# Loads of one weight moved to ScalarE's queue, and two fill products in place of five

## The chip, the cores and the metric

The kernel runs on one core of a Trainium2 chip. The metric is device time in microseconds (us) for one execution, taken from three runs of the same kernel. Five engines work beside each other: TensorE (PE in the profile, with its weight loads shown as PEld), VectorE (DVE), ScalarE (ACT), GpSimd (POOL) and SyncE (SP), which here only issues DMAs. DMAs can be issued by SP, by ACT and by POOL; a row such as "SPq ... DMA_DIRECT2D" in a timeline is the issue, not the transfer.

## The reference

For 8 samples of 1024 rows with 512 features, two conditioned residual layers follow each other:

```python
# layer 0: a base matrix plus a low-rank term made from the condition
ae = layernorm(cond) * ln_g + ln_b
h = gelu(ae @ w1 + b1)
x_a, x_b = split(h @ w2 + b2, 2)              # each (8, 512, 8)
layer = base[None] + einsum('bdr,bkr->bdk', x_a, x_b)
x = x + (x + einsum('btc,bco->bto', x, layer))
# layer 1: a weight scaled by the condition on its rows and normalised on its columns
ys = cond / sqrt(512)
d = rsqrt(einsum('bi,io->bo', ys * ys, W * W) + 1e-8)
x = x + einsum('bsi,io->bso', x * ys[:, None, :], W) * d[:, None, :]
```

The kernel multiplies the two layers into one 512 x 512 matrix for each sample and then applies that matrix once to x. For this it needs products of base (plus twice the identity) with W, scaled for each sample.

## The kernel before

Products are made in a 32-bit form that drops low bits, so each operand is split into a rounded part and a rest (`bh` and `bl` for base, an `nh` and an `nl` for W scaled by `ysT`), and each block product is the sum of three matrix products. Blocks are 128 rows; the inner dimension of 512 has four chunks, k = 0 to 3.

The setup comes first and the main stage after it. The setup makes the scaled norm `d`, the condition's layer norm `ae`, the small network (`w1`, then sixteen tiles of `w2`, 1 MB each, summed into `px`), the first base product `pg` for sample 0 and base products for samples 1 to 3. The main stage runs over 8 samples and 8 row blocks each; each step is twelve matrix products into `po`, a copy by ScalarE and a store issued by ScalarE. The base products and splits of later samples are woven between these steps.

The order of the setup is written out by hand. `mm` and `turn` (lines 44 to 48) pin TensorE's products and transposes to program order, and `ve`, `se` and `sy` (line 64) do the same for VectorE, ScalarE and SyncE. An engine that waits for one operand therefore holds back all that stands behind it.

The loads stand at lines 86 to 92, all on SyncE: `sm` (identity, the layer norm's parameters, the transposed condition: 86 KB), `cnd` (the condition, 16 KB), then by halves of 512 KB W (`w_sb`) and base transposed (`b_raw`) in turn, then `w1` (1 MB). The tiles of `w2` follow from `w2_group` (line 387), each of which issues a load ahead of four products; nine large buffers are shared (`big`, line 69), so later tiles wait until earlier buffers are free. Loads from SP and ACT share a small set of completion semaphores in program order; a load that takes a semaphore over waits until the earlier load with it has landed.

`keep_warm(count)` (line 106) issues products of a zero tile into a PSUM tile that nobody reads. Twelve of them (`WARM`) start the program on TensorE at line 111. Five more stand at line 256, between the transposes `pa` of the normalised condition and the first base products.

For the first base product (lines 257 to 259) these must be there: the first half of W, scaled and rounded by ScalarE (`round_yw`, lines 179 and 186, which stand behind ScalarE's square root of the layer norm at line 178); the first half of base, with twice the identity added by VectorE (`twice_i`, line 187) and then rounded, a quarter by VectorE (line 188) and three quarters by ScalarE (line 189).

Of the kernel before, what the change touches and what calls it, by code (L numbers as in the profile page):

```python
# [30 lines left out]
def cond_resid_kernel(ctx: ExitStack, tc: tile.TileContext, small, cond, condrows, consts,  # L31
# [10 lines left out]
    nc = tc.nc  # L42

    def mm(*args, **kw):
        tc.keep_in_program_order(nc.tensor.matmul(*args, **kw))  # L45

    def turn(*args):
        tc.keep_in_program_order(nc.tensor.transpose(*args))

    pin = tc.keep_in_program_order  # L50
# [13 lines left out]
    ve, se, sy = InOrder(nc.vector), InOrder(nc.scalar), InOrder(nc.sync)  # L64
# [16 lines left out]
    w_sb = cp.tile([P, KC, D], F32, name="w_sb")  # L81
# [4 lines left out]
    sy.dma_start(sm, small)  # L86
    sy.dma_start(cnd, cond)
    for at in (slice(0, 2), slice(2, 4)):
        sy.dma_start(w_sb[:, at, :], weight[:, at, :])
        sy.dma_start(b_raw[:, at, :], baseT[:, at, :])  # L90
    w1_sb = big_tile("w1_sb")
    sy.dma_start(w1_sb, w1)
# [13 lines left out]
    def keep_warm(count):  # L106
        for _ in range(count):
            mm(warm.rearrange("p (a c) -> p a c", c=P), zero,
               zero.unsqueeze(1).to_broadcast([P, D // P, P]), start=True, stop=True)
# [143 lines left out]
    pa = misc.tile([P, KC, NB], F32, tag="misc", name="pa")  # L253
    for k in range(KC):
        turn(pa[:, k, :], ae[:, k * P:(k + 1) * P], ident[:NB, :NB])
    keep_warm(5)
    for i, (s, m) in enumerate(((bh, n0[0][0]), (bh, n0[0][1]), (bl, n0[0][0]))):
        for c in range(KC):
            mm(pg[c], s[:, 0, c * P:(c + 1) * P], m, start=(i == 0), stop=False)
# [672 lines left out]
```

## Time and profile before

| | us |
|---|---|
| median of three runs | 305.82 |
| lowest and highest | 305.3 and 306.11 |
| the profiled execution | 305.47 |
| its span, from the first to the last instruction | 303.7 |

The span is cut into forty slices in the page. Busy shares are in tenths (9 is 90% or more), and the last two rows give the DMA engines' busy share and what they moved in GB/s:

```profile
PE   8999999999999999999999999999999999999995
DVE  4779830979678479977456478981266543600000
ACT  4756132256476564355664454743645546621221
DMA  6999999642319636631651134354151545322222
```

A slice is 7.6 us. TensorE is busy in all of them. The DMA engines are busy in the first seven or so, while the weights are loaded, and partly idle afterwards. The page's table of DMA issues names the loads around the change; its last column is the median time from issue to landing:

```profile
w<-in_w SPq DMA_DIRECT2D x16, 1024.0 KB, 11.1
...
w_sb<-in_weight SPq DMA_DIRECT2D x2, 512.0 KB, 5.4
b_raw<-in_baseT SPq DMA_DIRECT2D x2, 512.0 KB, 6.2
w_sb<-in_w SPq DMA_DIRECT2D x1, 1024.0 KB, 9.6
```

The sixteen rows named `w<-in_w` are the tiles of `w2`. The row `w_sb<-in_w` is the load of `w1`, whose name the profile gives in part only. In the rows of a timeline the first column is the start, the second the duration, and brackets hold the idle time of that engine just before and what ended it.

### The profile page before, as it was taken

How to read it: one execution, taken by the hardware profiler on the slowest of the kernel's cores; microseconds unless marked ns; L12 is line 12 of the kernel's file. 1: busy time of each engine (PE TensorE's matmuls, PEld its weight loads, DVE VectorE, ACT ScalarE, POOL GpSimd, SP SyncE). 2: the span in 40 equal slices, each digit the busy share in tenths (PEclk: the TensorE clock that was granted, in tenths of full speed). 3: DMA queues.
4: the chain of work that ended last, by engine and by line, in shares of the span. 5: the costliest groups of instructions: out<-in, count | busy, mean ns of one | idle time of the engine just before them, and what ended most of it. 6: DMA issues, size and time to landing. Idle time of an engine off the chain costs nothing.

```text
span 303.7 us, 3551 instructions
## 1 busy us (share of the span) xinstructions
PE 298.0 (98%) x1369; PEld 227.9 (75%) x1369; DVE 176.4 (58%) x262; ACT 145.9 (48%) x212; POOL 5.2 (2%) x14
## 2 busy tenths in 40 slices
PE   8999999999999999999999999999999999999995
PEld 3655565466888888888888888888888888888884
DVE  4779830979678479977456478981266543600000
ACT  4756132256476564355664454743645546621221
POOL 0011000001000000100000000000000000000000
PEclk9999999999999999999999999999999999999999
DMA  6999999642319636631651134354151545322222
GB/s 204 409 427 419 410 421 419 220 188 69 138 69 343 242 124 226 228 120 69 207 193 52 69 108 171 97 162 192 69 207 69 190 178 212 148 106 104 96 76 105
DMA packets 15952, 57.37 MB, mean 189 GB/s; under 512 B 1840, under 2 KB 2352, under 8 KB 11584
## 3 DMA queue, kind: packets, MB, share of 16 engines
q1 hardware_dynamic: 6064, 38.78, 34.5%
q10 hardware_dynamic: 9360, 16.78, 14.7%
q0 software_dynamic: 512, 1.59, 1.6%
q8 instruction: 10, 0.16, 0.2%
q14 instruction: 6, 0.05, 0.1%
HBM read 40.35 MB, written 16.79 MB: 188 GB/s over the span
## 4 chain that ended last, share of the span: by engine, by line
PE 88%; DVE 5%; DMA 4%; ACT 2%; issue 0%; ACTq 0%
PE po L45 57%; PE pp L45 13%; PE pq L45 7%; DMA w<-in_w 4%; PE px L45 3%; PE warm L45 2%; PE pg L45 2%; DVE n L62 2%; PE pr L45 2%; PE pt_t L45 1%; ACT work L62 1%; DVE scr L62 0%; PE ps_t L45 0%; DVE q L62 0%; PE pq_v L45 0%
## 5 line engine op out<-in xcount | busy, mean ns | idle before, releaser
L45 PE MATMUL po<-ph,xs 128*128 128x512 f32 (+1 forms) x520 | 164.2, 386 | 0.0
L45 PEld LDWEIGHTS po<-ph,xs 128*128 128x128 f32 x520 | 97.1, 188 | 19.8
L45 PE MATMUL po<-pl,xs 128*128 128x512 f32 (+1 forms) x260 | 100.3, 386 | 0.0
L62 ACT COPY o<-po 128x512 f32<-128x512 f32 (+1 forms) x65 | 37.8, 581 | 87.0 <-PE po L45 86.8
L45 PEld LDWEIGHTS po<-pl,xs 128*128 128x128 f32 x260 | 48.8, 188 | 9.9
L62 DVE TENSOR_TENSOR xs<-x,xs 128x1024 fp32r<-128x1024 f32 x32 | 38.7, 1221 | 20.5 <-ACT xs L62 20.5
L62 ACT CAST xs<-x 128x1024 fp32r<-128x1024 f32 x32 | 33.0, 1050 | 4.0 <-DMA x<-in_x 2.3
L62 DVE TENSOR_TENSOR nl_p<-n,nh_p 128x1024 fp32r<-128x1024 f32 x14 | 17.1, 1220 | 20.0 <-ACT nh_p L62 20.0
L62 DVE TENSOR_TENSOR pl<-q,ph 128x1024 fp32r<-128x1024 f32 x16 | 19.4, 1220 | 7.3 <-ACT ph L62 7.3
L62 DVE TENSOR_TENSOR q<-pr,q 128x512 f32<-128x512 f32 x24 | 15.8, 685 | 7.9 <-PE pr L45 7.8
L45 PE MATMUL pq<-nh,bh 128*128 128x512 f32 x48 | 19.8, 412 | 0.0
L45 PE MATMUL pq<-nl,bh 128*128 128x512 f32 x48 | 19.1, 398 | 0.1
L45 PE MATMUL pq<-nh,bl 128*128 128x512 f32 x48 | 19.0, 395 | 0.0
L62 ACT CAST ph<-q 128x1024 fp32r<-128x1024 f32 x16 | 16.6, 1051 | 3.9 <-DVE q L62 3.7
L62 DVE SCALAR_TENSOR_TENSOR n<-w_sb,ysT,d 128x512 f32<-128x512 f32 x24 | 17.8, 745 | 0.8 <-DMA d<-d_out 0.8
L62 ACT COPY q<-pp 128x512 f32<-128x512 f32 x20 | 11.7, 587 | 13.3 <-PE pp L45 13.3
L45 PE MATMUL px<-w,hT 128*32 128x512 f32 x128 | 16.0, 601 | 0.4 <-DMA w<-in_w 0.4
L62 ACT CAST nh_p<-n 128x1024 fp32r<-128x1024 f32 x14 | 14.7, 1052 | 2.5 <-PE pp L45 2.4
L45 PEld LDWEIGHTS pq<-nh,bh 128*128 128x128 f32 x48 | 9.0, 188 | 8.4 <-issue 5.0
L45 PE MATMUL pp<-nh_p,sh 128*128 128x512 f32 x32 | 12.4, 389 | 0.0
L45 PE MATMUL pp<-nl_p,sh 128*128 128x512 f32 x32 | 12.4, 389 | 0.0
L45 PE MATMUL pp<-nh_p,sl 128*128 128x512 f32 x32 | 12.4, 389 | 0.0
(135 smaller groups left out, 272.9 us busy)
## 6 DMA issues: line engine op xcount, KB each, us to landing
w<-in_w SPq DMA_DIRECT2D x16, 1024.0 KB, 11.1
x<-in_x SPq DMA_DIRECT2D x16, 1024.0 KB, 5.2
out<-o ACTq DMA_DIRECT2D x63, 256.0 KB, 2.0
d<-d_out POOLq DMA_DIRECT2D x6, 256.0 KB, 3.9
w_sb<-in_weight SPq DMA_DIRECT2D x2, 512.0 KB, 5.4
b_raw<-in_baseT SPq DMA_DIRECT2D x2, 512.0 KB, 6.2
w_sb<-in_w SPq DMA_DIRECT2D x1, 1024.0 KB, 9.6
b_nat<-in_base SPq DMA_DIRECT2D x1, 1024.0 KB, 9.5
```

What stands on the lines that cost most here:

```text
L45: tc.keep_in_program_order(nc.tensor.matmul(*args, **kw))
L62: return lambda *a, **kw: pin(f(*a, **kw)) if InOrder.on else f(*a, **kw)
```

## The change

The two loads of W are issued on ScalarE's queue, where they become its first instructions, in front of its table load. SyncE's queue keeps the small loads, base, `w1` and `w2` in the same order without W. The fill in front of the first base product has two products instead of five. Everything else, the order on VectorE and the rest of the order on TensorE included, stays.

```diff
     sy.dma_start(sm, small)
     sy.dma_start(cnd, cond)
     for at in (slice(0, 2), slice(2, 4)):
-        sy.dma_start(w_sb[:, at, :], weight[:, at, :])
+        pin(nc.scalar.dma_start(w_sb[:, at, :], weight[:, at, :]))
         sy.dma_start(b_raw[:, at, :], baseT[:, at, :])
     w1_sb = big_tile("w1_sb")
     sy.dma_start(w1_sb, w1)
...
         turn(pa[:, k, :], ae[:, k * P:(k + 1) * P], ident[:NB, :NB])
-    keep_warm(5)
+    keep_warm(2)
     for i, (s, m) in enumerate(((bh, n0[0][0]), (bh, n0[0][1]), (bl, n0[0][0]))):
```

Two semaphores move with it: W's first half takes the one that the small load had, and the load of the constants (`cst`, behind `w2`'s first tile on SyncE) now waits for that half of W where it waited for the small load.

## The prediction

> **What bounds the kernel now.** I read the page's busy shares first: TensorE is the bound, so only what moves TensorE's work earlier or later can count.
>
> ```profile
> PE 298.0 (98%) x1369; PEld 227.9 (75%) x1369; DVE 176.4 (58%) x262; ACT 145.9 (48%) x212; POOL 5.2 (2%) x14
> ```
>
> Of 303.7 us, TensorE sits idle for 5.7. Second, the list of waits of PE, to see where that idle time lies (columns: total us, times, longest us):
>
> ```profile
> PE warm L45 <- DVE eps_l L62: 1.0, 1, 1.0
> PE px L45 <- DMA w<-in_w: 0.4, 1, 0.4
> PE pd L45 <- DVE dst L62: 0.4, 1, 0.4
> ```
>
> One DMA wait in the whole run. Third, the timeline of 0 to 60 us, for what releases the first base product and for that wait:
>
> ```profile
> 1.57 0.35 SPq L62 DMA_DIRECT2D w_sb<-in_weight  x1
> 1.97 0.43 SPq L62 DMA_DIRECT2D b_raw<-in_baseT  x1
> ...
> 5.45 1.33 ACT L62 ACTIVATE nh<-w_sb,ysT 128x512 fp32r<-128x512 f32 x2 [1.44 <-DMA w_sb<-in_weight]
> ...
> 6.26 1.25 PE L45 MATMUL warm<-zero 128*128 128x512 bf16 x5
> 6.78 0.51 ACT L62 CAST bh<-b_raw 128x384 fp32r<-128x384 f32 x1
> 6.78 0.29 DVE L62 SCALAR_TENSOR_TENSOR b_raw<-sm,b_raw 128x128 f32<-128x128 f32 x1 [1.30 <-DMA b_raw<-in_baseT]
> ...
> 7.44 0.76 PEld L45 LDWEIGHTS pg<-nh,bh 128*128 128x128 f32 x4 [0.42 <-ACT bh L62]
> ...
> 48.03 1.06 PE L45 MATMUL px<-w,hT 128*32 128x512 f32 x8 [0.43 <-DMA w<-in_w]
> ```
>
> The first half of base (b0) lands at 6.78, ScalarE's rounding ends at 7.29, the first product's weights load at 7.44. ScalarE's own previous work (two roundings of W, from 5.45) also ends at 6.78, so both halves arrive together. The five fill products end at the same moment, 7.5: at present none of the three is slack. From 7.44 on TensorE is dense; at 48.03 it waits 0.43 us for a tile of w2 (the eleventh). Fourth, the windows, for the DMA stream (last two columns: DMA share, GB/s):
>
> ```profile
> 1.50:2.50 1.00, 1.00 (x4) 0.35 (x3) 0.00 (x0) 0.72 (x2) 0.00 (x0) 1.00 0.39 105
> 2.50:4.50 2.00, 2.00 (x6) 0.73 (x5) 1.49 (x7) 0.29 (x1) 0.00 (x0) 1.00 0.82 217
> 4.50:6.25 1.75, 1.75 (x9) 0.66 (x7) 0.87 (x4) 0.81 (x2) 0.00 (x0) 1.00 1.03 407
> 6.25:7.75 1.50, 1.50 (x8) 0.71 (x7) 0.94 (x4) 1.22 (x3) 0.00 (x0) 1.00 0.93 224
> ...
> 10.00:48.00 38.00, 37.08 (x207) 20.72 (x205) 26.27 (x60) 17.43 (x33) 2.53 (x5) 1.00 1.02 419
> ```
>
> From 10 to 48 us the stream runs full at 419 GB/s, so the tile awaited at 48.03 comes earlier only if the whole stream starts earlier. At the start there is room: up to 2.5 us just 105 KB move, which are the two small loads (86 + 16 KB); W's first half (W0), issued at 1.57, starts some 0.95 us after its issue.
>
> **What the Trainium skill says.** "DMA: Bandwidth & Descriptors", section "Issuing engines are not separate DMA queues": loads of SP and ACT run on the same 16 engines and interleave; several issuers save only issue time. The trace agrees for the full part (one queue alone reaches 419 GB/s), so I expect an earlier start, not a higher rate. The section "Queues, rings and completion order" of the same page: each engine takes turns between the two rings. The trace agrees only in part. A store of ACT issued 0.01 us after an x load landed with it; one issued 0.5 us after an x load landed after it had finished (both against 2.0 us for stores on their own):
>
> ```profile
> x<-in_x SPq DMA_DIRECT2D x1, 1024.0 KB, 5.6
> out<-o ACTq DMA_DIRECT2D x1, 256.0 KB, 5.8
> ```
>
> ```profile
> x<-in_x SPq DMA_DIRECT2D x1, 1024.0 KB, 5.2
> out<-o ACTq DMA_DIRECT2D x1, 256.0 KB, 5.4
> ```
>
> "Perfetto Trace Analysis", section "DMA Instruction — HWDGE (DVE, Sync)": the descriptor generator is shared and locked for one issuer. No issue in this trace shows a long lock wait (at 90.5 both queues issue together in 0.33 and 0.36 us). "TensorE: Matmul & The Clock Gate", "What's actually happening": an idle window of about 3.4 us drops the clock. The granted clock is 1.00 in all windows above; no gap in this trace is long enough to show it.
>
> **The change, part by part.** Call d the time by which the first base product comes earlier, and e the same for the DMA stream. At 48.03 the product of w2 starts at the later of TensorE's arrival (47.60 - d) and the tile (48.03 - e). After it TensorE is dense to the end (0.24 us idle from 60 to 290). So the gain is the smaller of 0.43 + d and e.
>
> *Three fill products removed.* 1.25 us / 5 = 0.25 each, 0.75 together. TensorE is then free at 6.26 + 0.50 = 6.76 instead of 7.51. Worth nothing if base is not earlier; it caps d at 7.44 - 6.76 = 0.68, and the gain at 0.43 + 0.68 = 1.11.
>
> *ScalarE's two issues.* Each some 0.35 to 0.43 (the rows of W and base on SP), in front of its table load (1.28 us from 0.74) and one small activation (0.20): that ends at about 1.5 + 1.28 + 0.20 = 3.0 instead of 2.23. Its next work is at 3.71, so 0.7 us of cover; cost 0.
>
> *e.* W0 is issued at 0.74 in place of 1.57: the stream starts 0.83 earlier. Lower bound 0.4 (if the generator takes the two small loads' issues, 0.37 each, in turn with W's); upper 1.3 (if the slow stretch 2.50 to 4.50, which loses 2.0 x (419 - 217)/419 = 0.96 us, halves because both tensors start together). I take 0.83. Later SP loads all move up too; consts now waits for the semaphore that W0 frees instead of the small load's, perhaps 0.3 us later than its issue at 4.76, and two loads of 1 MB, 5 us, are queued ahead of it: cost 0.
>
> *d, by base.* On SP b0 moves from 1.97 to 1.57, but W1 is now issued near 1.1, ahead of it. At best b0 follows the stream, 0.83 earlier, and the cap 0.68 holds. At worst all 512 KB of W1 pass first, as with the store issued 0.5 us late: 524 KB / 413 GB/s = 1.27 us, so b0 is 1.27 - 0.83 = 0.44 later.
>
> *d, by cond.* The small loads now share with W0. Cond stands behind up to 512 KB: at best 0, at worst 1.3 us. The layer norm follows it step by step (2.79 to 5.47), then the transposes pa (0.35), which precede the two fills. At present pa waits for the warm-up products until 5.91, 0.4 us after its operand, so a delay of 1.3 makes it 0.9 late: 6.76 + 0.9 = 7.66 for the first product, d = -0.2. ScalarE's square root waits too, but W0 covers it.
>
> So d lies between -0.44 and 0.68; I take the middle, +0.1. The gain: the smaller of 0.43 + 0.1 and 0.83, 0.53. Profiled execution: 305.47 - 0.53 = 304.94 (its span of 303.7 and 1.8 around it). The median of the three runs is 0.35 above that execution, so 305.3 on its scale. What is late next: at 48 TensorE itself again.
>
> **Rivals.**
> 1. *All cover holds, faster.* The small loads keep their turn and b0 comes with the earlier stream: d = 0.68, e at least 1.1, gain 1.1: 304.7. For it: the empty DMA before 2.5 us. Against: it needs e at its upper part, and no delay by W1.
> 2. *Base becomes the late one, slower.* b0 becomes the third half-megabyte instead of the second. The third load now, W1, was issued at 2.43 with 6.9 us to landing: 9.33. Less 0.83, b0 lands at 8.5, 1.7 later: d = -1.7, gain 0.43 - 1.7 = -1.3: 307.1. It decides as slower once b0 is later than 6.78 + 1.35 = 8.1. For it: the slow stretch 6.25 to 7.75 at 224 GB/s, which b0 escapes today. Against: nothing shows that this stretch belongs to the third place. A clock dropped in the then empty 1.7 us would add to it.
> 3. *The stream does not start earlier.* The generator takes issues in turn, e = 0.4 or less: gain 0 to 0.4, 305.4 to 305.8, no change.
>
> **How the numbers follow.** 0.3% is 0.92 us, about what a measurement of this kernel can tell. The forecast (gain -0.2 to 0.9) 0.36, rival 1 0.32, rival 2 0.22, rival 3 0.10. Rival 1 stands on the threshold, so a little more may fall beyond it from the forecast's upper end: faster 0.34, same 0.44, slower 0.22. Predicted 305.3. The forecast's own range is 304.9 to 306.0; with rival 1 less 0.2 for scatter 304.5, and up to most of rival 2, 307.0.
>
> **What would show it.** Right: W0's issue on ACT at 0.74; DMA over 200 GB/s before 2.5 us; the wait at 48 gone or under 0.4; the first base product near 7.3. For rival 1, that product at 6.8. For rival 2, base's wait on DVE ending past 8, a gap of TensorE after the two fills, and the 48 us product later than 48.03. Cond's statistics on VectorE (now 2.79) show how the small loads fared. Wrong altogether if TensorE shows a new wait after 60 us, or a clock below 1.00.

## The result, and the profile after

The changed kernel takes 308.0 us (median of six runs, 306.99 to 308.35) against 305.25 for the kernel before beside it: a ratio of 1.0077, interval 1.0058 to 1.0096. It is slower by 2.75 us, where 305.3 with a range of 304.5 to 307.0 was predicted. The profiled execution took 308.35, with a span of 306.4 against 303.7.

The page's busy shares and clock row for the changed kernel:

```profile
PE 298.7 (97%) x1366; PEld 228.6 (75%) x1366; DVE 176.4 (58%) x262; ACT 145.7 (48%) x212; POOL 5.1 (2%) x14
...
PEclk9799999999999999999999999999999999999999
```

The clock row of before:

```profile
PEclk9999999999999999999999999999999999999999
```

TensorE does three products fewer and is busy for 0.7 us more. The 7 in the second slice says that its clock was not full there; before, that row held nines only. TensorE's waits in the changed kernel (total us, times, longest):

```profile
PE pa L48 <- DVE scr L62: 2.0, 1, 2.0
PE warm L45 <- DVE eps_l L62: 1.0, 1, 1.0
PE pd L45 <- DVE dst L62: 0.3, 1, 0.3
PE pr L45 <- DVE q L62: 0.3, 1, 0.3
PE pg L45 <- DVE bh L62: 0.2, 1, 0.2
```

The wait for a tile of w2 is gone. In its place TensorE waits 2.0 us for the normalised condition, ahead of the fills, and 0.2 for base, behind them. The timeline of the changed kernel at its start, with issues on the two queues:

```profile
0.74 0.37 SPq L62 DMA_DIRECT2D sm<-in_small  x1
0.74 0.88 ACTq L89 DMA_DIRECT2D w_sb<-in_weight  x2
...
3.97 0.18 DVE L62 TENSOR_SCALAR ysT<-sm 128x32 f32<-128x32 f32 x1 [3.03 <-DMA sm<-in_small]
...
4.87 0.68 DVE L62 BATCH_NORM_STATS2 st<-scr 8x6 f32<-8x512 f32 x1 [0.72 <-DMA scr<-in_cond]
...
7.62 0.41 PE L48 MATMUL pa<-sm,scr 8*128 8x8 f32 x4 [1.95 <-DVE scr L62]
7.96 0.73 PE L45 MATMUL warm<-zero 128*128 128x512 bf16 x2
8.22 0.51 ACT L62 CAST bh<-b_raw 128x384 fp32r<-128x384 f32 x1 [0.91 <-DMA b_raw<-in_baseT]
...
8.92 2.05 PE L45 MATMUL pg<-nh,bh 128*128 128x512 f32 x4 [0.23 <-DVE bh L62]
```

The rows of before that these are read against, beside the rows of base in the prediction:

```profile
2.69 0.18 DVE L62 TENSOR_SCALAR ysT<-sm 128x32 f32<-128x32 f32 x1 [1.75 <-DMA sm<-in_small]
2.79 0.68 DVE L62 BATCH_NORM_STATS2 st<-scr 8x6 f32<-8x512 f32 x1
...
5.92 0.41 PE L48 MATMUL pa<-sm,scr 8*128 8x8 f32 x4
...
7.47 1.16 PE L45 MATMUL pg<-nh,bh 128*128 128x512 f32 x4
```

The small load reaches VectorE at 3.97 (2.69 before), cond at 4.87 (2.79), the transposes `pa` run at 7.62 (5.92), base lands at 8.22 (6.78), and the first base products start at 8.92 (7.47). Those four then take 2.05 us where they took 1.16. Windows of the changed kernel show why (length, busy time by engine, then clock, DMA share, GB/s); they are cut where the clock changed, and the first has the same length as the second:

```profile
4.90:8.31 3.41, 1.46 (x10) 0.58 (x8) 2.33 (x10) 1.61 (x4) 0.00 (x0) 1.00 0.98 359
8.31:11.73 3.42, 3.19 (x9) 2.27 (x8) 3.39 (x9) 3.14 (x7) 0.00 (x0) 0.50 1.04 438
11.73:15.00 3.27, 3.27 (x17) 2.18 (x19) 2.80 (x7) 1.85 (x3) 0.16 (x1) 1.00 1.01 416
```

In the first window TensorE was busy for 1.46 of 3.41 us, and for the next 3.42 it ran at half clock. How late TensorE was further on is read from two more products, `pq_v` behind the base products and the last one of the run, first before and then changed:

```profile
11.82 1.07 PE L45 MATMUL pq_v<-wsq,ysq 128*32 128x512 f32 x8
...
299.93 0.28 PE L45 MATMUL po<-ph,xs 128*128 128x256 f32 x1
```

```profile
14.56 1.07 PE L45 MATMUL pq_v<-wsq,ysq 128*32 128x512 f32 x8
...
302.40 0.28 PE L45 MATMUL po<-ph,xs 128*128 128x256 f32 x1
```

From the first base product to `pq_v` it took 11.82 - 7.47 = 4.35 us before, and now 14.56 - 8.92 = 5.64: 1.29 more. So TensorE was 1.45 late by the first base product and 2.74 late at `pq_v`. The wait of 0.43 at the w2 tile, which is gone, gives that much back. In the last matrix product of the run the lag is 302.40 - 299.93 = 2.47 us.

### The profile page after: what moved, and what is told of

The parts are those of the page before. It is cut to its first block, busy times and chain, and to the rows that moved or that the text cites. A ratio compares the mean times of both kernels' runs of the same rounds, so it can differ in the third digit from the quotient of the medians.

```text
span 306.4 us, 3545 instructions
## 1 busy us (share of the span) xinstructions
PE 298.7 (97%) x1366; PEld 228.6 (75%) x1366; DVE 176.4 (58%) x262; ACT 145.7 (48%) x212; POOL 5.1 (2%) x14
## 4 chain that ended last, share of the span: by engine, by line
PE 89%; DVE 5%; DMA 2%; ACT 1%; issue 1%; SPq 0%; ACTq 0%
PE po L45 57%; PE pp L45 13%; PE pq L45 9%; PE px L45 4%; PE pg L45 2%; DMA b_raw<-in_baseT 2%; DVE n L62 2%; PE pr L45 2%; PE pt_t L45 1%; ACT work L62 1%; DVE scr L62 0%; PE ps_t L45 0%; DVE q L62 0%; PE pq_v L45 0%; ACT nh L62 0%
## 5 line engine op out<-in xcount | busy, mean ns | idle before, releaser
L62 ACT CAST nh<-n 128x512 fp32r<-128x512 f32 (+1 forms) x10 | 6.9, 708 | 12.9 <-DVE n L62 12.9
```

Source lines behind the costliest of these rows:

```text
L62: return lambda *a, **kw: pin(f(*a, **kw)) if InOrder.on else f(*a, **kw)
```

## The experiments

My theory after the result, A: a load issued about 0.4 us later than another waits for all of that one's packets, on whichever queue; cond thus stands behind the first half of W, base behind both halves, and the wait for cond leaves TensorE idle enough for its clock to halve. The rivals were the removed fills, the use of two queues in itself, and an early issue on ScalarE.

**Each part alone.** The loads on ScalarE's queue with five fills kept:

```diff
-    keep_warm(2)
+    keep_warm(5)
```

> The loads of W on ScalarE's queue, all five fill products kept. Theory A (issue order: cond stands behind the first half of W, base behind both halves, and TensorE's clock halves while it waits for cond): the fills are not what costs; the statistics start near 4.9 us, base lands near 8.2, the clock drops all the same, and the three extra fills run at half clock in front of a base that has come, so 308 to 309 us, 1.0 to 1.2% above the kernel before. Theory B (the clock drops because three fills were taken out): clock at full, first product near 8.9, 306.7 us or less.

Measured: 309.62 us, ratio 1.0128 (1.0106 to 1.0151), somewhat above the range of A; B falls. The windows of this run (same columns) show the clock at half for twice as long:

```profile
4.03:7.44 3.41, 1.21 (x6) 0.35 (x4) 2.10 (x10) 1.43 (x3) 0.00 (x0) 1.00 0.98 365
7.44:10.85 3.41, 3.02 (x10) 1.75 (x11) 2.94 (x8) 2.45 (x6) 0.00 (x0) 0.50 1.02 428
10.85:14.27 3.42, 3.42 (x9) 2.64 (x8) 3.39 (x10) 2.71 (x5) 0.00 (x0) 0.50 1.02 424
```

The five fills ran at half clock from 8.36 and pushed the first base products to 10.11, although base had landed at 8.21. With these loads, fewer fills are the better choice: 308.0 against 309.6.

The fills alone, with all loads on SyncE as before:

```diff
-    keep_warm(5)
+    keep_warm(2)
```

> All loads on SyncE, two fill products in place of five. Theory A: TensorE stands idle for some 0.7 us in front of the first base product and nothing else moves: first product at 7.4, time within 0.3% of before. Theory B: the clock drops here too, 1.3 us or more lost, 306.6 us or above.

Measured: 305.1 us, ratio 1.0003 (0.9989 to 1.0018). The time is as A expects, although base itself came later in this trace (7.03) and the first base product at 7.73 after a wait of 0.52. With the loads in their old order the fills cost and gain nothing that can be told from none, so the loss comes with the loads.

**The clock's share.** The changed kernel with TensorE kept busy from the start until cond is there:

```diff
-WARM = 12
+WARM = 19
```

> The changed kernel with 19 instead of 12 products of zeros at the very start, so that TensorE is busy until cond's transposes can begin (near 7.6 us). Theory A: no second stretch at half clock; the late base alone remains, first product near 8.9, 1.45 later than before, less the 0.43 us wait at 48: 306.3 to 306.7 us, some 1.3 below the changed kernel. Theory C (the clock's dip costs nothing, the late base is all): 308 as the changed kernel.

Measured: 306.89 us, ratio 1.0052 (1.0037 to 1.0066): 1.1 below the changed kernel, with the clock at 1.00 in the window that ran at half clock there. The two rows show TensorE busy through the window before, and then the clock, for this run:

```profile
4.90:8.31 3.41, 3.41 (x14) 1.25 (x13) 2.52 (x10) 1.78 (x4) 0.00 (x0) 1.00 1.03 394
8.31:11.73 3.42, 3.42 (x19) 2.72 (x19) 3.39 (x9) 3.14 (x7) 0.00 (x0) 1.00 1.02 432
```

It is a little above the range of A, but C falls. Of the remaining 1.6 us (0.5%), the trace shows TensorE 1.28 late at the first base products (8.75) and 1.12 late at its last product (301.05 against 299.93); what the rest is stays open. The changed kernel's own runs show the same split: the one whose mean clock was 0.998 took 306.99, the five with 0.992 or 0.993 took 307.81 to 308.35.

**What makes base late.** The second half of W goes back to SyncE, behind base's first half:

```diff
-        pin(nc.scalar.dma_start(w_sb[:, at, :], weight[:, at, :]))
+        by = se if at.start == 0 else sy
+        by.dma_start(w_sb[:, at, :], weight[:, at, :])
```

> As the changed kernel (two fills), but only the first half of W on ScalarE's queue; the second half goes back to SyncE, behind the first half of base. Theory A (a load issued later waits for what the other queue issued before): base has only the first half of W ahead of it and lands 1.2 to 1.4 us earlier than in the changed kernel, near 6.9; cond is as late as there (statistics near 4.9), so the transposes stay near 7.6, the first base product comes near 8.3, the clock still drops: 307.2 to 307.7 us. Theory E (the two queues share by turns, and base is late for another reason): base still lands near 8.2, 308 us.

Measured: 307.7 us, ratio 1.0078 (1.0056 to 1.01). The first base load's row in the table of DMA issues, of the changed kernel and of this run (last column: us to landing), issued at 1.58 and 1.57:

```profile
b_raw<-in_baseT SPq DMA_DIRECT2D x1, 512.0 KB, 6.6
```

```profile
b_raw<-in_baseT SPq DMA_DIRECT2D x1, 512.0 KB, 4.8
```

Base lands 1.8 us sooner after its issue with nothing moved but the second half of W: E falls. Cond stays late (statistics at 4.94), `pa` stays at 7.68, and the first base products start at 8.28. In the profiled execution the clock held, and it is the lowest of fourteen times (306.08 to 310.14); the clock had risen later there (the twelve warm-up products took 5.30 us, against 4.68 in the changed kernel), so that the wait for cond was shorter, 1.4 us. The median, 307.7 against 308.0, says that base alone repaired gains little as long as cond is late.

**What makes cond late.** One queue only, the first half of W issued first:

```diff
+    sy.dma_start(w_sb[:, first, :], weight[:, first, :])
     sy.dma_start(sm, small)
     sy.dma_start(cnd, cond)
     sy.dma_start(b_raw[:, first, :], baseT[:, first, :])
+    sy.dma_start(w_sb[:, second, :], weight[:, second, :])
```

> All loads on SyncE and five fills as before, but the first half of W is issued ahead of the two small loads. Theory A (order of issue alone makes cond late, whichever queue): the small loads land behind the first half of W, statistics at 4.5 us or later, transposes at 7.3 or later, the clock drops: 307 to 309 us although base is in its old place. Theory F (two queues beside each other are what hurts): statistics below 3.5, time within 0.3% of before.

Measured: 308.3 us, ratio 1.0088 (1.0057 to 1.0119), with this timeline:

```profile
5.01 0.18 DVE L62 TENSOR_SCALAR ysT<-sm 128x32 f32<-128x32 f32 x1 [4.07 <-DMA sm<-in_small]
5.10 0.68 DVE L62 BATCH_NORM_STATS2 st<-scr 8x6 f32<-8x512 f32 x1
...
7.84 0.41 PE L48 MATMUL pa<-sm,scr 8*128 8x8 f32 x4 [1.60 <-DVE scr L62]
```

Cond is as late, and the loss as large, without ScalarE's queue. So it is the order of issue and not the second queue: F falls. Then the changed kernel with its two small loads exchanged:

```diff
-    sy.dma_start(sm, small)
     sy.dma_start(cnd, cond)
+    sy.dma_start(sm, small)
```

> The changed kernel with the two small loads on SyncE in the other order, cond (one packet on each of eight DMA engines) ahead of the 86 KB load (eight packets on each engine). Theory A with turns (each DMA engine takes packets of the two queues in turn while both were issued together, and what is issued later waits): cond lands with the first packets of W, the 86 KB load as late as before or a little later (scaling at 4.0 to 4.3); the statistics follow the scaling at 4.2 to 4.5 in place of 4.87, the transposes come near 7.1, and base stays last near 8.2: 307 to 308 us, the clock drops in fewer executions. Theory G (all small loads wait until the first half of W is through): statistics at 4.8 or later again, 308 us or more.

Measured: 308.47 us, ratio 1.0109 (1.0072 to 1.0146). The numbers are those of G, but neither theory had the mechanism right. What SyncE's queue (q1) moved from 1.60 to 2.40 us (packets, MB, share of 16 engines), and the rows for the 86 KB load, issued at 1.19 behind W's issue at 0.74:

```profile
q1 hardware_dynamic: 16, 0.02, 13.8%
...
sm<-in_small SPq DMA_DIRECT2D x1, 86.0 KB, 4.1
...
5.29 0.18 DVE L62 TENSOR_SCALAR ysT<-sm 128x32 f32<-128x32 f32 x1 [4.35 <-DMA sm<-in_small]
5.38 0.67 DVE L62 BATCH_NORM_STATS2 st<-scr 8x6 f32<-8x512 f32 x1
```

Cond was there: the 0.02 MB are its 16 KB, moved before 2.40, and the statistics ran 0.09 us after the scaling, with no wait for a DMA. But VectorE takes the scaling first, and the 86 KB load, now the later one, took 4.1 us from its issue. In the changed kernel, issued in the same moment as W, it took 3.2, and before, with nothing ahead of it, 1.9. So a load issued 0.45 us later did not share with the earlier one packet by packet; it waited for nearly all of it.

**A way to keep the early start.** Only the 16 KB load of cond goes to ScalarE's queue, so that nothing large comes ahead of a small load and W is issued 0.4 us earlier:

```diff
-    sy.dma_start(cnd, cond)
+    pin(nc.scalar.dma_start(cnd, cond))
```

> The kernel before with only the 16 KB load of cond on ScalarE's queue; W, base and five fills as before. Theory A: cond arrives beside the other small load, ahead of W; W and all that follows on SyncE are issued 0.4 us earlier, the tile of w2 awaited at 48 comes 0.4 earlier: 304.9 us, 0.1% faster (0 to 0.2%). Theory D (any load issued first by ScalarE delays the start, through its table load): statistics later than 2.8, first product later than 7.44, time above before by 0.3 us or more.

Measured: 306.69 us, ratio 1.0044 (1.0026 to 1.0062), with times from 305.23 to 309.6. D's numbers came true (statistics at 2.93, the first base products at 8.61, 1.4 us lost), but its mechanism is not shown: the run with the fills alone has its statistics at 2.93 too, with all loads on SyncE. What was late is the first half of W: it took until 6.20, where it was there at 5.45 before, although issued 0.40 us earlier. A repetition on another chip:

> The kernel with only cond on ScalarE's queue a second time, for a second trace and more times on another chip. Theory D (an early load on ScalarE's queue makes the start of the stream slower): median again 0.3% or more above before, first half of W landing at 6.0 or later, first base product at 8.3 or later. Theory H (the first trace showed one of the stream's slow starts, which before has too): median within 0.2% of before.

Measured: 306.14 us, ratio 1.0028 (1.0008 to 1.0048); W at 6.09, first base products at 8.03. That lies between D and H. The w2 tile came later too: TensorE waited for it until 48.95. The traces cannot decide: the run with the late base copy, below, starts with its loads in the old order, and in its trace W comes at 6.07 and the first base products at 8.03 as well. The loss is measured in the times of both runs (42 executions); its cause stays open. Issuing W earlier did not move its arrival forward in either.

**Two tries at a faster kernel.** First, the wait at 48 us taken away, by loading the second copy of base (1 MB) one w2 tile later:

```diff
-        if len(todo) == 6:
+        if len(todo) == 5:
```

> The kernel before, with one edit: the 1 MB load of base for the later addition is issued after the eleventh tile of w2 instead of ahead of it. By the sum of the prediction the gain is the smaller of 0.43 + d and e; here d = 0 and e = 2.5 us (1 MB at 419 GB/s), so the wait at 48 goes and 0.0 to 0.43 us are gained: 304.9 us, 0.1%. If the addition then waits for its base (used at 55.8), the gain is lost: 305.3 or above.

Measured: 305.65 us, ratio 1.0001 (0.9986 to 1.0016). There was no wait for w2 in its profile, and no gain that could be told from none. But TensorE was itself 0.56 late at the first base products there (8.03), so the trace does not show that the edit took the wait away. The wait is not in each execution of the old order either: the run with two fills alone had none, and its tile was used from 47.79 on, 0.24 earlier than in the trace of before. Then with W and base in quarters and two fills on top:

```diff
-    for at in (slice(0, 2), slice(2, 4)):
+    for at in (slice(0, 1), slice(1, 2), slice(2, 4)):
...
-    keep_warm(5)
+    keep_warm(2)
```

ScalarE and VectorE do the first quarter's work ahead of the second's in that kernel.

> The edit of the run before it (late base copy), all loads on SyncE, the first halves of W and base loaded in quarters in turn (W0, base0, W1, base1), ScalarE's and VectorE's work on the first quarter ahead of the second, two fills. By the prediction's sum d = 0.5 to 0.68 with e = 2.5: gain 0.9 to 1.1 us, first base product at 6.8 to 7.0, 304.3 us, 0.3% faster. Rival: two more issues on SyncE and smaller packets slow the slow start of the stream further, base's second quarter comes after 7.5 and holds the products of k = 1: no gain, 305.3.

Measured: 305.46 us, ratio 0.999 (0.9974 to 1.0005), no clear gain. In its profiled execution, which took 306.94, the first base products started at 7.49 only, and the window from 2.50 to 4.50 us moved 130 GB/s, where the kernel before moved 217, which is the slower start that the rival named. No kernel here beats the one before by more than its interval.

## Why the prediction was wrong

*The form held, two terms did not.* The gain was written as the smaller of 0.43 + d and e. The first step that failed is the size of d, taken as +0.1 between -0.44 and 0.68: the first base product came 1.45 later. The second is the clock, which was read as 1.00 and priced at nothing: it cost 1.29 us between that product and `pq_v`. With both, the sum is 0.43 - 1.45 - 1.29 = -2.31. The lag at the last product is 2.47; most of the difference comes at a later product `pr`, where TensorE now waits 0.28 us for VectorE and the lag grows from 2.31 to 2.44.

*The stream, e.* The windows of the changed kernel, and the one of before that the prediction does not show:

```profile
1.50:2.50 1.00, 1.00 (x4) 0.34 (x3) 0.00 (x0) 0.84 (x1) 0.00 (x0) 1.00 0.46 72
2.50:4.50 2.00, 2.00 (x6) 0.73 (x5) 0.18 (x1) 0.64 (x2) 0.00 (x0) 1.00 0.99 321
4.50:6.25 1.75, 1.17 (x5) 0.27 (x3) 1.12 (x4) 0.46 (x2) 0.00 (x0) 1.00 1.04 412
6.25:7.75 1.50, 0.13 (x2) 0.13 (x3) 1.14 (x6) 1.06 (x2) 0.00 (x0) 1.00 0.91 295
7.75:10.00 2.25, 2.02 (x9) 1.22 (x9) 1.75 (x5) 1.51 (x3) 0.00 (x0) 0.63 1.03 431
10.00:48.00 38.00, 37.55 (x201) 22.13 (x200) 27.59 (x62) 18.47 (x35) 2.49 (x5) 0.98 0.96 385
```

```profile
7.75:10.00 2.25, 2.25 (x11) 1.82 (x10) 2.25 (x5) 2.13 (x5) 0.00 (x0) 1.00 1.03 391
```

From 1.5 to 10 us the changed kernel moved 2.85 MB against 2.47 (each window's length times its GB/s, added), 0.38 MB or 0.9 us at 419 GB/s, where I took 0.83. The size was right, but not for the reason given. Before 2.5 us less was moved than before (72 against 105 KB), and by 6.25 the lead was 1.44 against 1.25 MB, 0.44 us; the other half came later, where the old kernel's stream was the slower one (224 and 391 GB/s against 295 and 431). At the tile, e can't be read: from 10 to 48 us the changed kernel moved 385 GB/s against 419, and TensorE came late to the tile.

*d, by base.* I had the mechanism, base behind the second half of W, and priced it at 524 KB / 413 GB/s = 1.27, less the earlier start of 0.83: 0.44 late at worst. It was 1.44 late. Of the missing 1.00, the lead accounts for 0.39 (0.44 at 6.25 us instead of 0.83), and the rate for 0.43 by estimate: 413 GB/s is the later stream's, and from 6.25 to 7.75, while base was on its way, the changed kernel moved only 295. Rival 2, which took the landing of the third half-megabyte from the trace itself, said 8.5; it was 8.22. Nearest in time was that rival, at 307.1, with 0.22. It named a drop of the clock as a possible addition without a price, and put it in a gap behind the fills, which came to 0.23 us only.

*d, by cond.* I allowed a delay of 1.3 us at most, half a megabyte at the later stream's rate. It was 2.08: cond stood behind the first half of W while the stream was still at 72 and then 321 GB/s, and the 86 KB load, which itself came 1.28 later, shared that stretch. `pa` moved by 1.70, not by 0.9. Cond by itself held TensorE until 8.69, when the two fills ended; base then set the start at 8.92.

*The clock.* I read a clock of 1.00 and no gap that was long enough, in the trace of before. The gap that the change opened was in front of the fills: warm-up products end at 5.66 and `pa` begins at 7.62. My own bound of 0.9 for a late `pa` had put an idle stretch there, and I didn't ask what it does to the clock. It cost 1.29 us in the trace, and 1.1 in the run with more warm-up products. "TensorE: Matmul & The Clock Gate", section "What's actually happening", speaks of an idle window of about 3.4 us. Here the half clock did last 3.42, but 1.96 us without work inside one such window were enough to bring it.

*Fills, ScalarE's issues, later loads.* Right, by the runs and the trace: the fills alone made no difference (1.0003), ScalarE's table load and small activation ended at 3.15 with its next work at 5.79, and the constants came 1.1 us earlier than before (14.84 against 15.98 on GpSimd).

*The skill's turns.* I took "Queues, rings and completion order" (of "DMA: Bandwidth & Descriptors") for half of the truth, since one of two stores in the trace spoke against it, and then chose the middle of the bounds. The runs say that the later store was the case to follow. The section also gives the size of a turn, which I left out: an engine drains a whole packet, typically 9 to 17 descriptors, from one ring before it switches. What ScalarE's queue (q10) moved up to 8 us are the two halves of W:

```profile
q10 hardware_dynamic: 288, 1.05, 36.7%
```

The profile's 288 packets are 128 of 4 KB for each half, eight for each of 16 engines, and 16 small ones at its end. Turns of the size that the page gives would let such a half pass as a whole. So the order measured here doesn't contradict the page, and no run here separates such turns from plain order of issue.

## What to carry to other kernels

Before a large load is issued earlier, list the small loads that it overtakes, and follow each to the engine that waits for it: moving two loads to another queue made 100 KB late by 1.3 to 2.1 us. Price a place in the line from landings of the same stretch of the same trace, not from the full rate of a later one. A gap of TensorE can cost twice: here the late start was 1.45 us, and the fall of the clock that the gap brought added 1.29. Ask for the clock at each gap the change opens, in front of fill products as well as behind them.

## What was not expected of the hardware

Two loads issued in the same moment on two queues shared the DMA engines, but one issued 0.40 to 0.45 us later waited for nearly all of the first, half a megabyte: cond behind W (4.87 against 2.79 us), base behind the second half of W (6.6 us to landing against 4.8), the 86 KB load behind W (4.1 against 1.9 us).

And the clock rises at a time of its own in each execution: the twelve warm-up products, started at 0.99 us, took 4.21 us in one trace and 5.30 in others, since they start 0.43 us apart at first and 0.22 apart after the rise. (A trace's record of the clock begins with the rise, at 3.95 to 6.96 us in these traces. The windows give 1.00 before it as well, and that figure says nothing about the clock there.) What a wait for cond costs depends on how much of it lies behind the rise. In the four traces in which the clock fell, it fell 3.41 or 3.42 us after it had risen, and TensorE had been busy for 1.21 to 1.80 us of these; in the other traces it was busy for at least 2.52 us of that stretch, and the clock held. The two cases next to each other are the run with W first on SyncE, which waited for 1.6 us, all behind the rise, and the run with half of W on ScalarE, which waited for 1.4 us, of which 0.9 lay behind the rise:

```profile
6.05:9.46 3.41, 1.80 (x11) 1.10 (x11) 3.02 (x12) 2.92 (x6) 0.00 (x0) 1.00 0.99 312
9.46:12.87 3.41, 3.41 (x9) 2.63 (x9) 3.38 (x10) 3.28 (x7) 0.00 (x0) 0.50 1.01 428
```

```profile
6.79:10.20 3.41, 2.52 (x14) 2.04 (x15) 3.31 (x10) 2.87 (x6) 0.00 (x0) 1.00 1.01 398
```

Where between 1.80 and 2.52 the border lies was not measured.
